# A three-stage convolution block: a written-out opening for the third stage with direct mean and variance products, first products ahead of a transpose, and other buffers for the last pieces

## The chip, the cores and the metric

The kernel runs on one core of one Trainium2 chip. The number that counts is the device time of one execution in microseconds (us), taken as the median of the runs shown. A core has a matrix engine (TensorE, "PE" in the profile, with "PEld" for its weight loads), a vector engine (VectorE, "DVE"), an activation engine (ScalarE, "ACT"), GpSimd ("POOL") and a synchronising engine ("SP"). SP, ACT and POOL also issue the DMA transfers. Each engine carries out its own instructions in the order written and waits on semaphores for the others.

## What is computed

The input is `x` of shape (16, 192, 64, 64), float32. Two layers follow each other (weights are cut away here):

```python
def layer0(x):
    h = ln2d(x)                                    # over the 192 channels, for every pixel
    projected, gate = split(conv1x1(h, in_proj))   # 192 -> 2 * 192
    projected = dwconv3(projected)                 # depthwise 3x3
    scanned = scan_lr + scan_rl + scan_tb + scan_bt    # four first-order recurrences, weighted
    mixed = (scanned + dwconv3(projected)) * sigmoid(gate)
    mixed = gelu(batch_norm(mixed))                # statistics over images and pixels
    x = x + conv1x1(mixed, out_proj)
    m = conv1x1(gelu(conv1x1(ln2d(x), fc1)), fc2)  # 192 -> 768 -> 192
    return x + m

def layer1(x):
    t = relu(bn(mean(x, pixels) @ w1.T))           # per image
    taps = (t @ w2.T + b2) * MASK                  # 4 taps of 9 are left by the mask
    return depthwise3x3(x, taps) + bias            # own taps for each image and channel
```

## The kernel before

The instruction order of all engines is the order of the Python text. The images are taken in eight pairs, one image on each half of the 128 partitions, with the 192 channels as three groups (`t` = 0, 1, 2) of 64.

**First stage** (lines 246 to 584): 64 chunks `n` of 512 pixels of a pair, four quarters `g` each. `load_a` brings a chunk (three transfers on SP, three on POOL), three chunks ahead. `turn(n)` transposes it on PE into PSUM (one buffer, `ps_xt`), `variance(n, g)` reads the per-pixel statistics from there on DVE, `deviation(n)` makes the reciprocal of the deviation, and `project(n)` multiplies by the weights `wi` into `ps_pj` (two buffers of each kind); DVE (line 517) and ACT (line 518) scale the two images' results into a staging block. The mean is taken out of the weights beforehand: `projection_weights` scales `wi`, makes its column means on PE (line 281) and subtracts them on DVE (line 284). Loop order: `turn(n + 1)`, then `project(n)` with the statistics of `n + 1` among its quarters. Four chunks make a block; blocks lie alternately in `stg` and in `mid`, and during the next block the four stores of a block go out on POOL and SP. So the first write of a block waits for the stores of the block two before. The table `side` puts small steps after given chunks: the weight loads after 40, 41, 43 and 44, and after chunks 46, 47, 48 and 49 `load_dm(0)`, `load_lm(0)`, `load_dm(1)`, `load_lm(1)`, which bring banded matrices for the second stage, each on SP for one half of the partitions and on POOL for the other (786 KB for a `dm`, 655 KB for a `lm`, by their tile shapes).

**Second stage** (587 to 789): 24 groups of eight channels; depthwise product, two scans on DVE, local product, gate. At the end of a group its result, 2 MB, goes to DRAM (`mixed_d`, line 704, one transfer on POOL). The last group lies in `mid`. For it, four small transfers (702) first put what chunk 0 of the next stage needs directly in its place. Then `spread` and `batch_norm` make the statistics while the DVE transposes (`turn_back`, 239) turn chunk 0.

**Third stage** (792 to 1096): 64 chunks `n` of 512 pixels again. The steps of a chunk:

- `unmix` (transposes, DVE), `bn_gelu` (852 and 853, ACT) make `mx`: parts 0 and 1 with 128 channels, part 2 with the other 64 channels;
- `out_proj(n, t)`: products over part 2 (880, "quarters" below) and then parts 0 and 1 (884, "columns"); `residual(n, t)` (890, DVE) adds the input into the image `ximg`; for `t` = 1 and 2 it also adds up the channels by thirds and halves (894, 905);
- `mean` (913): four products of these sums with a constant matrix; `center` (920) subtracts the mean; `squares` (927 ACT, 928 and 905 DVE) squares and adds; `mean` again for the variance;
- `normalize`: square root (936, ACT, with an activation-table load), `reciprocal` (939) and product (940) on DVE;
- `first(n, k)` for `k` = 0, 1, 2 (952, PE; GELU 954 on ACT) and `second(n, k)` (825 by way of `both`, PE); `final` (972) adds to the image.

The loop runs from `n` = -3 and overlaps four chunks: `first(n, 0)`, `products(n, 0)` (mean of `n + 1` and output product 0 of `n + 2`), `squares(n + 1)`, the last `second` of `n - 1`, `first(n, 1)`, `products(n, 1)` (variance of `n + 1`), `second(n, 0)`, `normalize(n + 1)`, `first(n, 2)`, `products(n, 2)`, `second(n, 1)`. The opening is the same loop with the missing chunks left out. In `products` mean and output product share a PSUM tile, `ps_o` ("f1", two buffers, also used by `first`). `load_y` brings `mixed_d` back, two chunks at a time; in the opening into the room of `ximg1`, which is empty until the second pair.

**The end** (1098 to 1118): the depthwise product of the last pair, twelve pieces of 1024 pixels and 64 channels. Five are made on ACT and DVE (1026 and 65), seven on PE (1035) with an eviction on ACT (1037). All twelve write into the four `gl` buffers in turn, and a buffer is free again when its transfer to DRAM has ended.

Of the kernel before, what the change touches and what calls it, by code (L numbers as in the profile page):

```python
# [27 lines left out]
C = 192  # L28
# [27 lines left out]
def conv_block_kernel(ctx: ExitStack, tc: tile.TileContext, x, prm, w_in, w_out, w_fc1, b_fc1, w_fc2, w1, bn1, w2, out):  # L56
# [103 lines left out]
    early = ExitStack()  # L160
    ce = early.enter_context(tc.tile_pool(name="early", bufs=1))
    ones = ce.tile([128, 128], F32, tag="ones", name="ones")

# [10 lines left out]
    mats[0]["lm"] = lm_even  # L174

    SB_ = 2 * 2 * C * BR
    mid = ce.tile([128, SB_], F32, tag="mid", name="mid")
    mats[1]["lm"] = mid[:, NPG:NPG + 5 * HW * (GC // 2)].rearrange("p (k m c) -> p k m c", k=5, m=HW)
# [67 lines left out]
    with ExitStack() as stage:  # L246
# [199 lines left out]
        for k in (0, 1, 3, 4):  # L446
            beside(40 + k, load_weights, k)
        beside(46, load_dm, 0)
        beside(47, load_lm, 0)
        beside(48, load_dm, 1)  # L450
        beside(49, load_lm, 1)
        beside(50, squeeze_scale)
# [46 lines left out]

        def project(n):  # L500
            blk, part = divmod(n, per)
            if part == 0:
                if blk % 2:
                    both_i = mid.rearrange("p (i o j) -> p i o j", i=2, j=BR)
                else:
                    both_i = stg.tile([128, 2, 2 * C, BR], F32, tag="stg", name="stg")
                stag[blk] = [both_i[:, i] for i in range(2)]
            for g in range(AR):
                ps = [psa.tile([128, 2 * C], F32, tag=f"pj{i}", name=f"ps_pj{i}", bufs=2) for i in range(2)]
                for t in range(3):  # L510
                    for i, q in enumerate(HALF):
                        nc.tensor.matmul(ps[i], pixels(n, t, g)[q], wi[q, t].rearrange("p g k c -> p (g k c)"),  # L512
                                         start=(t == 0), stop=(t == 2))
                if n + 1 < n_ac:
                    variance(n + 1, g)
                j, rs = part * AR + g, ast[n]["rs"]
                nc.vector.tensor_scalar_mul(stag[blk][0][:, :, j], ps[0], rs[:, g, 0:1])  # L517
                nc.scalar.activation(stag[blk][1][:, :, j], ps[1], AF.Copy, scale=rs[:, g, 1:2])  # L518
# [36 lines left out]
        next(steps)  # L555
        decays()
        turn(0)
        next(steps)
        for g in range(AR):
            variance(0, g)  # L560
        next(steps)
        deviation(0)

        for n in range(n_ac):
            if n + 3 < n_ac:
                load_a(n + 3)
            blk, part = divmod(n, per)
            if blk:
                if part == 0:
                    store_first(blk - 1)  # L570
                    store(blk - 1, 0, (nc.gpsimd, nc.sync))
                store(blk - 1, part + 1, (nc.gpsimd, nc.sync))
                if part == per - 1:
                    stag.pop(blk - 1)
            if n + 1 < n_ac:
                turn(n + 1)
            project(n)
            if n + 1 < n_ac:
                deviation(n + 1)
            for f, args in side.pop(n, ()):  # L580
                f(*args)
# [5 lines left out]
    with ExitStack() as stage:  # L587
# [98 lines left out]
        def gate(k):  # L686
# [9 lines left out]
            if c == hp_ - 1:  # L696
                if g == NCG - 1:

                    for i in range(2):
                        for wh in range(2):  # L700
                            w0_ = 32 * wh
                            (nc.sync, nc.gpsimd)[wh].dma_start(y_low[2 * w0_ + 32:2 * w0_ + 64, 2, i, LASTC * BR:],
                                                              s["pg"][w0_:w0_ + 32, i * NB, 0].rearrange("p c j -> p (c j)"))
                nc.gpsimd.dma_start(mixed_d[:, :, :, g].rearrange("i b p e -> p (i b) e"),
                                    s["pg"][:, :, 0].rearrange("p n c j -> p n (c j)"))
                s.clear()
# [89 lines left out]
    n_img = 2  # L796
    ximg = [k3.tile([128, 3, HW + 1, RW], F32, tag=f"ximg{i}", name=f"ximg{i}") for i in range(n_img)]

# [56 lines left out]
    def products(n, t):  # L855
# [4 lines left out]
        ps = ps2.tile([128, 2, CH], F32, tag="f1", name="ps_o", bufs=2)  # L860
        pm, po = ps[:, :, HCH:CH], ps[:, :, 0:HCH]
        if t < 2:
# [11 lines left out]
    def out_proj(n, t, ps):  # L874

        s = st[n]

        for wh, qr in enumerate(HALF):
            for i, q in enumerate(HALF):
                nc.tensor.matmul(ps[q, wh], wo2[qr, 64 * t:64 * t + 64], s["mx"][qr, 2, 256 * i:256 * i + 256],  # L880
                                 start=True, stop=False)
        for wh in range(2):
            for i, q in enumerate(HALF):
                nc.tensor.matmul(ps[q, wh].rearrange("p (r w) -> p r w", w=32), wo[:, 64 * t:64 * t + 64],  # L884
                                 cols(rows(s["mx"][:, i]))[:, :, wh], start=False, stop=True)

    def residual(n, t, ps):
        s, img = st[n], img_of(n)
        for wh in range(2):
            nc.vector.scalar_tensor_tensor(cols(img[:, t])[:, :, wh], ps[:, wh].rearrange("p (r w) -> p r w", w=32),  # L890
                                           pt3[:, t, OUTB:OUTB + 1], cols(rows(s["x2"][:, t]))[:, :, wh], ALU.add, ALU.add)
        if t == 1:
            s["sum"] = hp2.tile([128, 3, HCH], F32, tag="sm", name="sm", bufs=1)
            nc.vector.tensor_add(rows(s["sum"][:, 0:2].rearrange("p k n -> p (k n)")), img[:, 0], img[:, 1])
# [12 lines left out]
    def mean(n, ps, what):  # L907
# [3 lines left out]
        for k, kinds in enumerate(((s0, sx), (sx, s1))):  # L911
            for i, a in enumerate(kinds):
                nc.tensor.matmul(ps[HALF[i], k], mean64[HALF[k]], a[HALF[k]], start=True, stop=True)  # L913

    def center(n, pm):
# [101 lines left out]
    def dynamic_last(p, g, t, dg, queues=(nc.gpsimd, nc.sync)):  # L1017

        xi, taps, r = ximg[p % n_img], pst[p]["taps"], g * GR
        o = wp.tile([128, GR, HW], F32, tag="gl", name="ol", bufs=4)  # L1020
        src = lambda k, r0, nr: xi[:, t, r0 + k // 3:r0 + k // 3 + nr, k % 3:k % 3 + HW]
# [34 lines left out]

    for n in range(-3, n_ch + 1):
        ended = (n - 1) // NCH if n >= NCH and (n - 1) % NCH == NCH - 1 else None
        if n + 5 < NCH and (n + 5) % 2 == 0:
            load_y(n + 5, ys[(n + 5) // 2], (nc.sync, nc.gpsimd) if n == -3 else (nc.gpsimd,))  # L1060
        if n == -3:
            border(ximg[0])
        if n == 0:
            nc.vector.memset(pool2, 0.0)
        if n == NCH - 3:
            border(ximg[1])

        early_, late_ = (n + 3, None) if n != -1 else (None, 2)
        at(load, n + 3)
        at(unmix, early_)  # L1070
        at(load_mixed, n + 4)
        at(first, n, 0)
        at(bn_gelu, early_)
        products(n, 0)
# [19 lines left out]
        at(second, n, 1)  # L1094
        at(unmix, late_)
        at(bn_gelu, late_)

# [63 lines left out]
```

## Time and profile before

| | us |
|---|---|
| three runs | 3748.33, 3750.83, 3751.44; median 3750.83 |
| profiled execution | 3738.29, of which 3736.5 are the span of the profile |
| first stage, about | 0 to 636 |
| second stage, about | 636 to 1311 |
| third stage, about | 1311 to 3697 |
| end, about | 3697 to 3736.5 |
| busy over the span: PE, DVE, ACT, POOL | 3686.8, 2706.0, 1786.6, 420.2 |

The profile is of one execution. A line of a timeline has the start, the length, the engine, the line of the code, the operation with its operands, the number of merged instructions, and in brackets how long the engine was idle before and for whom it waited. A float32 matmul shows as two instructions. A line of windows has the bounds, the length, then busy time and number of instructions of each engine, the granted share of the TensorE clock, the DMA engines' share and GB/s.

### The profile page before, as it was taken

What the parts mean: (1) busy time and instruction counts of PE and PEld (TensorE: products, weight loads), DVE (VectorE), ACT (ScalarE), POOL (GpSimd) and SP (SyncE); (2) the same over time, 40 slices, a digit from 0 to 9 for tenths busy, and PEclk for the clock granted to TensorE, in tenths of its full rate; (3) what the DMA queues carried; (4) which work ended last, traced back from release to release, by engine and by line L of the source; (5) the groups of instructions that cost most, each with busy time, mean ns of one, the idle gap of its engine ahead of it and who ended that gap; (6) DMA issues with size and microseconds to landing.
All of it is one profiled execution on the core that took longest, in us unless ns stands there. A gap on an engine that the chain in (4) does not pass through costs nothing.

```text
span 3736.5 us, 71017 instructions
## 1 busy us (share of the span) xinstructions
PE 3686.8 (99%) x30252; PEld 1649.4 (44%) x30252; DVE 2706.0 (72%) x4164; ACT 1786.6 (48%) x1945; POOL 420.2 (11%) x683
## 2 busy tenths in 40 slices
PE   8999999999999979999999999999999999999998
PEld 5666656555555533333333333333333333333333
DVE  6887776999999965557666766766766766675763
ACT  3434434888888833334334434434443443443432
POOL 2334332101011020000000000000000000000000
PEclk9999999999999989999999999999999999999999
DMA  6899997999999841112212222222222221221212
GB/s 163 241 252 243 265 280 238 308 294 283 280 283 271 226 100 27 51 44 63 78 56 66 69 67 62 69 61 68 74 57 58 76 71 42 80 75 43 69 37 74
DMA packets 308427, 491.74 MB, mean 132 GB/s; under 512 B 46656, under 2 KB 202640, under 8 KB 308112
## 3 DMA queue, kind: packets, MB, share of 16 engines
q1 hardware_dynamic: 250064, 295.14, 29.5%
q0 software_dynamic: 57152, 190.94, 18.7%
q8 instruction: 239, 3.92, 0.4%
q10 hardware_dynamic: 896, 1.12, 0.1%
q14 instruction: 76, 0.62, 0.1%
HBM read 284.91 MB, written 197.92 MB: 129 GB/s over the span
## 4 chain that ended last, share of the span: by engine, by line
PE 96%; DMA 2%; DVE 1%; SPq 0%; POOL 0%; issue 0%; ACT 0%; ACTq 0%; DVEq 0%; POOLq 0%
PE ps_f L952 27%; PE ps_f L825 27%; PE ps_pj L512 12%; PE ps_l L662 11%; PE ps_d L618 7%; PE ps_o L884 5%; PE ps_xt L484 2%; PE ps_o L880 2%; PE ps_o L913 1%; DMA xa<-in_x_dram 1%; PE ps_k L825 0%; DMA ximg<-mixed_d 0%; DMA mixed_d<-mid 0%; SPq L472 0%; PE ps_d L1035 0%
## 5 line engine op out<-in xcount | busy, mean ns | idle before, releaser
L954 ACT ACTIVATE gl<-ps_f,bf 128x1024 f32<-128x1024 f32 x384 | 427.6, 1114 | 1316.2 <-PE ps_f L952 1316.2
L952 PE MATMUL ps_f<-h,wf 64*64 64x512 f32 x9216 | 1035.8, 594 | 6.8 <-DVE h L940 6.7
L825 PE MATMUL ps_f<-gl,place 128*64 128x512 f32 x4608 | 1022.2, 592 | 0.0
L952 PEld LDWEIGHTS ps_f<-h,wf 64*64 64x64 f32 x9216 | 334.5, 133 | 693.8 <-issue 642.6
L825 PEld LDWEIGHTS ps_f<-gl,place 128*64 128x64 f32 x4608 | 334.2, 137 | 574.5 <-issue 533.4
L512 PE MATMUL ps_pj<-wi,xa 64*128 64x384 f32 x3072 | 515.6, 488 | 3.5 <-DVE stg L517 3.5
L920 DVE TENSOR_TENSOR h<-ximg,ps_o 128x768 f32<-128x768 f32 x128 | 116.4, 951 | 425.3 <-PE ps_o L884 417.0
L512 PEld LDWEIGHTS ps_pj<-wi,xa 64*128 64x128 f32 x3072 | 294.3, 187 | 196.8 <-issue 12.2
L890 DVE SCALAR_TENSOR_TENSOR ximg<-ps_o,pt,low 128x256 f32<-128x256 f32 x384 | 168.0, 479 | 266.8 <-PE ps_o L884 266.8
L65 DVE SCALAR_TENSOR_TENSOR o<-ximg,taps,o 128x1024 f32<-128x1024 f32 x252 | 323.2, 1282 | 9.1 <-ACT o L1011 2.6
L1015 POOL DMA_DIRECT2D out_dram<-o x168 | 87.9, 528 | 2067.6 <-DVE o L65 2064.8
L939 DVE RECIPROCAL rs<-rs 128x512 f32<-128x512 f32 x64 | 214.3, 3349 | 27.0 <-ACT rs L936 27.0
L653 DVE TENSOR_TENSOR_SCAN v<-tab,q 128x1024 f32<-128x1024 f32 x96 | 218.3, 2274 | 6.8 <-ACT tab L641 6.8
L655 DVE TENSOR_TENSOR_SCAN v<-tab,q 128x1024 f32<-128x1024 f32 x96 | 217.5, 2266 | 0.0
L518 ACT ACTIVATE stg<-ps_pj,rsa 128x384 f32<-128x384 f32 x128 | 120.5, 945 | 188.7 <-PE ps_pj L512 178.5
L884 PE MATMUL ps_o<-low,wo 128*64 128x256 f32 x1536 | 210.0, 395 | 0.0
L641 ACT ACTIVATE tab<-mask,dec_b 128x1024 f32<-128x1024 f32 x192 | 209.8, 1146 | 0.0
L518 ACT ACTIVATE mid<-ps_pj,rsa 128x384 f32<-128x384 f32 x128 | 120.8, 944 | 181.7 <-PE ps_pj L512 174.7
L491 DVE BATCH_NORM_STATS2 st<-ps_xt 128x6 f32<-128x192 f32 x512 | 173.8, 340 | 17.3 <-PE ps_xt L484 17.1
L239 DVE STREAM_TRANSPOSE low<-low 128x512 f32<-128x512 f32 x174 | 167.7, 1016 | 2.1 <-issue 0.3
L972 DVE SCALAR_TENSOR_TENSOR ximg<-ps_f,pt,ximg 128x512 f32<-128x512 f32 x192 | 134.4, 749 | 40.2 <-PE ps_f L825 37.8
L472 POOL DMA_DIRECT2D xa<-in_x_dram x192 | 119.8, 630 | 362.6 <-PE ps_pj L512 285.0
(197 smaller groups left out, 4060.1 us busy)
## 6 DMA issues: line engine op xcount, KB each, us to landing
low<-in_x_dram SPq DMA_DIRECT2D x128, 384.0 KB
out_dram<-o POOLq DMA_DIRECT2D x168, 256.0 KB, 3.7
mid<-pg_d SPq DMA_DIRECT2D x8, 4096.0 KB
low<-mixed_d SPq DMA_DIRECT2D x116, 256.0 KB
low<-pg_d SPq DMA_DIRECT2D x7, 4096.0 KB
pg_o<-pg_d SPq DMA_DIRECT2D x7, 4096.0 KB
xa<-in_x_dram POOLq DMA_DIRECT2D x192, 128.0 KB, 5.6
xa<-in_x_dram SPq DMA_DIRECT2D x192, 128.0 KB
```

The source lines that it names most:

```text
L65: nc.vector.scalar_tensor_tensor(o, in0, scalar, in1, ALU.mult, ALU.add, **kw)
L512: nc.tensor.matmul(ps[i], pixels(n, t, g)[q], wi[q, t].rearrange("p g k c -> p (g k c)"), start=(t == 0), stop=(t == 2))
L518: nc.scalar.activation(stag[blk][1][:, :, j], ps[1], AF.Copy, scale=rs[:, g, 1:2])
L618: nc.tensor.matmul(dst(ps[o, ih]), mats[g % 2]["dm"][q, di + 1, :, ch], src(s["pg"][q, :, 0, ch]), start=(di == 0), stop=stop)
L653: nc.vector.tensor_tensor_scan(vf, tab, q, 0.0, ALU.mult, ALU.add)
L655: nc.vector.tensor_tensor_scan(vf[:, ::-1], tab[:, ::-1], q[:, ::-1], 0.0, ALU.mult, ALU.add)
L662: nc.tensor.matmul(dst(bst[k]["ps"][o, i]), lm_of(g)[q, m, :, c], src(q, ih), start=start, stop=stop)
L825: nc.tensor.matmul(ps[q], w(i), rhs(i), start=start, stop=stop)
L884: nc.tensor.matmul(ps[q, wh].rearrange("p (r w) -> p r w", w=32), wo[:, 64 * t:64 * t + 64], cols(rows(s["mx"][:, i]))[:, :, wh], start=Fa ...
L939: nc.vector.reciprocal(rs, rs)
L952: nc.tensor.matmul(pf[o, i], wf1[q, t, m0:m0 + 64], s["h"][q, t], start=(t == 0), stop=(t == 2))
L954: nc.scalar.activation(gl, pf, AF.Gelu, bias=bf1[:, m:m + 1])
```

## The change

- First stage: the means of `wi` are made and subtracted before `turn(0)`. For chunk 0 the first two quarters are projected before `turn(1)`, the other two after it with two statistics steps each. `load_dm` and `load_lm` stand after chunks 46, 48, 50, 52, in the order dm 0, lm 0, dm 1, lm 1.
- `mid` is the first tile of its pool, and `ximg1` is placed before `ximg0`. In the built program `mid` then has the addresses of `ximg1`, and no address in common with `ximg0`.
- The 2 MB store of the last group is two transfers of 1 MB, one on SP and one on POOL.
- The third stage's loop starts at `n` = 1. What lay before is written out. For chunk 0 the columns stand before the quarters, and the sums on DVE are left out: mean and variance come from twelve products each, straight from the image and from the squares. They have a PSUM bank of their own. The squares are made in two halves, and the square-root table is loaded right after them. `normalize(0)` stands before `residual(1, 1)` on DVE.
- The pieces of the end that ACT and DVE make write into the `o` buffers (three pieces) and the `h2` buffers (two); the four `gl` buffers are left to the seven PE pieces.

```diff
@@ first stage
-        beside(46, load_dm, 0)
-        beside(47, load_lm, 0)
-        beside(48, load_dm, 1)
-        beside(49, load_lm, 1)
+        for i in range(2):
+            beside(46 + 4 * i, load_dm, i)
+            beside(48 + 4 * i, load_lm, i)
...
         decays()
+        next(steps)
+        next(steps)
         turn(0)
-        next(steps)
         for g in range(AR):
             variance(0, g)
-        next(steps)
         deviation(0)
...
+            h = AR // 2 if n == 0 else 0
+            project(n, range(h), lambda g: ())
             if n + 1 < n_ac:
                 turn(n + 1)
-            project(n)
+            project(n, range(h, AR), lambda g: (g,) if h == 0 else (2 * (g - h), 2 * (g - h) + 1))
@@ store of the last group
+                parts = ((nc.gpsimd, 0, n_half),) if g < NCG - 1 else ((nc.sync, 0, n_half // 2), (nc.gpsimd, n_half // 2, n_half))
+                for queue, i0, i1 in parts:
+                    queue.dma_start(mixed_d[i0:i1, :, :, g].rearrange("i b p e -> p (i b) e"),
+                                    s["pg"][:, i0 * NB:i1 * NB, 0].rearrange("p n c j -> p n (c j)"))
@@ third stage
+    def mean_part(n, pm, t, k, src):
+        for i, q in enumerate(HALF):
+            nc.tensor.matmul(pm[q, k], mean64[q], src[q], start=(t == 0 and k == 0), stop=(t == 2 and k == 1))
...
+    load_y(2, ys[1], (nc.sync, nc.gpsimd))
+    border(ximg[0])
+    for n in range(2):
+        load(n)
+        unmix(n)
+        bn_gelu(n)
...
+    for t in range(3):
+        out_alone(0, t)
+        if t:
+            for k in range(2):
+                mean_part(0, pm, t - 1, k, img0[:, t - 1, halves[k]])
+    for k in range(2):
+        mean_part(0, pm, 2, k, img0[:, 2, halves[k]])
+    center(0, pm)
+    load(2)
...
+    for k in range(2):
+        nc.scalar.activation(sq0[:, k], st[0]["h"].rearrange("p t (k n) -> p k t n", k=2)[:, k], AF.Square)
+    nc.scalar.activation(warm, eps6, AF.Sqrt)
+    out_alone(1, 0)
+    pw = one_bank()
+    for k in range(2):
+        for t in range(3):
+            mean_part(0, pw, t, k, sq0[:, k, t])
+    st[0]["pw"] = pw
+    normalize(0)
+    load_y(4, ys[2], (nc.gpsimd,))
+    residual(1, 1, out_alone(1, 1, True))
+    out_alone(1, 2)
+    first(0, 0)
+    pm = ps2.tile([128, 2, CH], F32, tag="f1", name="ps_o", bufs=2)[:, :, 0:HCH]
+    mean(1, pm, "sm")
+    unmix(2)
+    center(1, pm)
+    bn_gelu(2)
+    squares(1)
+    load(3)
+    first(0, 1)
+    unmix(3)
+    out_alone(2, 0)
+    second(0, 0)
+    bn_gelu(3)
+    products(0, 1)
+    normalize(1)
+    first(0, 2)
+    products(0, 2)
+    second(0, 1)
+    nc.vector.memset(pool2, 0.0)
+
+    for n in range(1, n_ch + 1):
@@ the end, dynamic_last
+        if dg is None:
+            o = (op.tile([128, GR, HW], F32, tag="o", name="o") if g < 2 else
+                 hp2.tile([128, 3, CH], F32, tag="h2", name="ol")[:, 0:2].rearrange("p k (h w) -> p (k h) w", w=HW))
+        else:
+            o = wp.tile([128, GR, HW], F32, tag="gl", name="ol", bufs=4)
```

`out_alone` is an output product with its residual (without it where `later` is set, in two `f2` banks of its own).

## The prediction

> **What bounds the kernel now.** I read the busy shares first: PE 99%, so only idle or slowed PE time can be won. Then windows by stage, to find where it idles:
>
> ```profile
> 21.50:300.00 278.50, 278.45 (x1805) 176.52 (x1804) 222.65 (x724) 111.20 (x149) 100.82 (x169) 1.00 0.83 219
> 430.00:500.00 70.00, 66.62 (x412) 42.19 (x410) 48.16 (x144) 25.69 (x35) 27.56 (x47) 0.98 0.97 282
> 1300.00:1320.00 20.00, 10.89 (x92) 6.13 (x89) 17.40 (x23) 9.87 (x10) 2.81 (x3) 0.72 0.42 113
> 1320.00:1345.00 25.00, 15.07 (x102) 6.43 (x98) 13.76 (x24) 5.77 (x7) 14.58 (x27) 0.81 0.82 167
> 1400.00:3640.00 2240.00, 2240.00 (x17430) 829.43 (x17426) 1475.54 (x2046) 905.35 (x871) 87.98 (x169) 1.00 0.23 61
> 3640.00:3736.50 96.50, 85.41 (x650) 31.61 (x642) 37.79 (x53) 29.27 (x27) 5.18 (x10) 0.94 0.26 75
> ```
>
> The second column of numbers is the length, the third PE's busy time: no gap in 1400 to 3640, and the order there is untouched. What can move lies at 9 to 30, at 430 to 500, at 1306 to 1348 and after 3697. Third, PE's and DVE's timelines through the opening of the third stage:
>
> ```profile
> 1318.18 1.13 PE L880 MATMUL ps_o<-low,wo 64*64 64x256 f32 x8 [3.84 <-ACT low L853]
> 1326.56 1.69 PE L913 MATMUL ps_o<-sm,mean 64*64 64x256 f32 x7 [1.53 <-DVE sm L905]
> 1334.69 1.95 PE L913 MATMUL ps_o<-sq,mean 64*64 64x256 f32 x6 [4.79 <-DVE sq L905]
> 1340.30 1.08 PE L884 MATMUL ps_o<-low,wo 128*64 128x256 f32 x8
> 1348.09 7.91 PE L952 MATMUL ps_f<-h,wf 64*64 64x512 f32 x48 [6.71 <-DVE h L940]
> 1371.08 5.38 PE L952 MATMUL ps_f<-h,wf 64*64 64x512 f32 x48
> ...
> 1321.80 0.88 DVE L890 SCALAR_TENSOR_TENSOR ximg<-ps_o,pt,low 128x256 f32<-128x256 f32 x2 [2.02 <-PE ps_o L884]
> 1329.96 1.82 DVE L920 TENSOR_TENSOR h<-ximg,ps_o 128x768 f32<-128x768 f32 x2 [2.19 <-PE ps_o L884]
> 1342.79 3.35 DVE L939 RECIPROCAL rs<-rs 128x512 f32<-128x512 f32 x1 [1.36 <-ACT rs L936]
> ```
>
> PE waits on one dependent chain for chunk 0: products, residual, mean, centre, squares, variance, root, reciprocal. It ends at 1348.09, and the first 48 instructions then take 7.91 us instead of 5.38. The other two places, PE in the first stage and ACT at the end:
>
> ```profile
> 489.60 5.83 PE L512 MATMUL ps_pj<-wi,xa 64*128 64x384 f32 x24 [3.04 <-DVE stg L517]
> ```
> ```profile
> 3730.58 1.11 ACT L1037 ACTIVATE ol<-ps_d,pt 128x1024 f32<-128x1024 f32 x1 [2.75 <-DMA out_dram<-ol]
> ```
>
> The first waits for a staging block whose last store was issued by SP at 480.14 and landed at 488.62 (chain of waits); the second for a `gl` buffer.
>
> **Part A, first chunk: -2.4 us.** Now the six mean products start when the weights are scaled (9.23) instead of at 14.61: 9.3 + 4.2 (the row of line 281) = 13.5. The last piece of chunk 0 is in at 13.46 (chain), so `turn(0)` follows: 2.8 (the row of 12 transposes at 18.75) gives 16.3; with 1.53 (warm row at 29.69) or 3.26 (three cold rows of 1.09) it would be 15.0 or 16.8. Eight statistics steps of 0.47: 20.1. Meanwhile PE makes two quarters, 24 instructions of 0.167 (8.01 for 48): 20.3; `turn(1)` to 21.8, its input having been there at 18.75 before. Root and reciprocal (0.6), two scalings (0.9 each) to 22.5, four statistics steps 24.4, scaling 25.3, four steps 27.2. `turn(2)` begins at 27.3, against 29.69. Ends: 3.7, and 0 if the next chunks are not in that early.
>
> **Part B, the banded matrices: -2.0 us.** `load_lm(0)` moves from after chunk 47 to after 48, `load_dm(1)` to 50, `load_lm(1)` to 52. On SP and POOL they now pass the loads and stores of these chunks, each of which goes out one or two transfers earlier. The matrices are first used from 640 on, over 100 us later. The late store at 480.14 stood behind the same SP transfers, but POOL's half of `lm` 0 (327 KB, issued at 474.91) no longer shares the DMA with it: 327 KB at 282 GB/s is 1.2 us. The clock's share of this stall is 5.83 - 4.14 (the same 24 at 334.73) = 1.7; after an idle time of 0.41 nothing of it was paid, after 3.04 all, so I take half, 0.85. Ends: 0 and 3.04 + 1.7 = 4.7.
>
> **Part C, the opening: -8.2 us.** Columns first: they need only line 852 (ends 1317.42), where the quarters needed 853 (1318.13): -0.7. Three products lasted from 1318.18 to 1325.02, 6.84; one set of four mean products now stands among them. A set puts two products on the array at a time, as line 884 does (1.01 warm), so 1.01; bounds 0.43 (eight of line 913) and 1.95. 1317.47 + 6.84 + 1.01 = 1325.3; the second set to 1326.3 while DVE makes the last residual (0.88); third set 1327.35; centre at 1327.45, against 1329.96. The store of `mid` does not matter much here: the first residual began at 1321.80 because that store ended at 1321.71, and in the built program it still lists a wait for both halves, though the addresses are now apart; it has slack, since the set that needs it starts at 1322.6. The split itself I cost at nothing: in 1315 to 1319 the DMA share was already 0.97 and 1.00.
>
> Then: first half of the centre 0.95, 1328.4; half square 0.9 (between 0.80 for 512 elements at line 853 and 1.24 for 1024), 1329.3, the other 1330.2; variance products 1.5 each half (three pairs of 0.5), 1330.9 and 1332.4; the table load (1.28 + 0.2) ends at 1331.7 beneath them; root 0.69 to 1333.2; reciprocal 3.35, product 1.76 and 0.1 between them: 1338.4. `first(0, 0)` starts at 1338.5 instead of 1348.09: -9.6. Cover for the longer variance products: nothing, they are on the path; the sums they replace (0.69 + 1.77 twice) were too. The residuals of chunk 1 now stand behind the product on DVE.
>
> What is late next: `first(0, 1)` has only `mean(1)` (0.43) before it where mean and output product stood, and its PSUM buffer waits for the GELU of the second half: 1.1 + 0.2 - 0.43 = 0.9 lost. `unmix(2)` stands ahead of `center(1)` on DVE, with the second buffer of `first(0, 1)` behind it: residuals, sums and transposes 0.88 + 0.69 + 0.88 + 1.77 + 3.0 = 7.2, to 1345.6, centre to 1347.5; PE wants that buffer at about 1350. Without `second(0, 0)` between, the second buffer of `first(0, 2)` waits for the root of chunk 1: about 0.5. So 9.6 - 1.4 = 8.2. PE idles from 1335.4 (two output products after 1332.4) to 1338.5, 3.1 us; I assume that the clock falls, as in this row after 3.04. Ends: 5.1 (mean and variance sets at the cold rate, + 3.1) and 12.5 (sets at 0.43, and the clock stays up).
>
> The Trainium skill ("TensorE: Matmul & The Clock Gate", Part 1) says that the clock falls after an idle window of about 3.4 us. By that rule 3.1 us of idleness would leave it up and the sum would be 2.65 larger, 17.4; the first-stage row above (3.04 idle, then slow) decides for me.
>
> **Part D, the end: -2.2 us.** Seven PE pieces need PE from 3701.95; four took 15.52, to 3717.47, and three at 3.58 end at 3728.2 without the gaps 0.17 and 0.64 at 3717.64 and 3725.38. The last eviction then starts at 3728.3 instead of 3730.58, and the 4.8 us from its end to the span's end stay. SP gets the stores of the DVE pieces earlier, and their fifth ends near 3724.7, ahead of that. Ends: 0.8 and 2.3.
>
> **Sum.** 2.4 + 2.0 + 8.2 + 2.2 = 14.8. Against the profiled execution 3738.29 - 14.8 = 3723.5; the median of the runs lies 12.5 higher, which I carry over: 3750.83 - 14.8 = **3736.0 us**.
>
> **Rivals.**
> - *The clock stays up* before `first(0, 0)`: 2.65 more, and the half cold price in B, 0.85: 3732.5. For it: 3.1 is an estimate, and in 1306 to 1309 the clock share was 0.98 with PE idle from 1306.4. Against: 0.50 from 1309 on, 2.6 us after.
> - *The clock stays down through the whole opening*: C falls to 5.1, and the late warm-up costs another 2.5 in `first(0, 1)`: total 9.2, 3741.6. Against: 1.00 in 1324 to 1332 with fewer products.
> - *The opening's gain is handed back to the transfers* of `load_y(2)`: `unmix(2)` asks at 1342.6, not at 1350.57, and holds `center(1)` behind it. Were the data there only at 1350.5, C would be nothing, 6.6 would be left, 3744.2: no change. Against: these 24 transfers landed 2.5 to 3.6 us after issue, the last about 1332. The same holds if the built order leaves the old wait on the path.
> - *Slower*: the matrices moved to chunks 50 and 52 meet the stores of the next blocks, and PE stalls at each block boundary, chunks 48, 52, 56 and 60, for 8.0 each, halfway between the stall of before (4.7) and the longest transfer in the chain of that stage (11.34, `xa` at 303.30): 32.0 - 4.7 = +27.3, less A, C and D (12.8), +14.5: 3765.3. It decides from a DMA share near 1.0 after chunk 48 on; 500 to 636 shows 0.83 and 243 GB/s, which should drain.
>
> **Chances.** Forecast 0.57, clock up 0.18, clock down 0.10, handed back 0.08, slower 0.07. A difference below 0.2% (7.5 us) can't be told from no change here. Faster is the first three, 0.85; same 0.09 (the fourth, and a mild form of the last); slower 0.06. The range 3728 to 3745 takes in the ends of all four parts but for their coincidence, and all cases but the last.
>
> **What would show it.** Right: first `ps_f` product near 1338 less what A and B moved it (about 1334), twelve-product sets near 1.0 each four, no idle PE beyond 1 us until the steady rhythm, no wait for `out_dram<-ol` at line 1037's counterpart, a stall after chunk 48 below 2 us. Wrong: a DMA wait ahead of `turn(1)`, new waits for `stg` or `mid` at later blocks, or DVE waiting for `ximg<-mixed_d`.

## The result and the profile after

| | before | after |
|---|---|---|
| runs, median (lowest to highest), us | 3749.58 (3746.79 to 3751.44), 4 runs | 3725.53 (3720.6 to 3734.31), 4 runs |
| profiled execution, us (its span) | 3738.29 (3736.5) | 3720.6 (3718.8) |

The ratio is 0.9939, 95% interval [0.9918, 0.996]: faster by 24 us, and by 15 to 31 with the interval. A second group of runs with another copy of the same kernel gave 3727.87 (5 runs) against 3746.5 (9 runs), 0.9949 [0.9937, 0.9962], so 14 to 24 us. The prediction had the sign and the places right and said 14.8; the time lies 2.5 below the low end of its range.

The windows of the kernel after, in the columns explained for before (bounds, length, busy time and instructions of PE, PEld, DVE, ACT and POOL, clock, DMA share, GB/s):

```profile
21.50:300.00 278.50, 277.77 (x1804) 176.32 (x1804) 223.14 (x732) 110.27 (x150) 104.18 (x173) 1.00 0.86 224
300.00:360.00 60.00, 57.68 (x364) 35.90 (x362) 42.45 (x125) 22.98 (x32) 22.91 (x38) 0.97 1.03 249
430.00:500.00 70.00, 69.88 (x447) 43.22 (x444) 52.95 (x158) 28.38 (x38) 26.41 (x46) 1.00 1.01 292
1314.92:1339.92 25.00, 21.30 (x184) 10.33 (x180) 16.89 (x24) 7.27 (x10) 14.93 (x27) 0.89 0.91 164
1400.00:3625.00 2225.00, 2225.00 (x17308) 823.60 (x17308) 1467.95 (x2041) 898.88 (x864) 88.12 (x169) 1.00 0.23 61
```

430 to 500 has lost its gap (66.62 of 70 busy before), and the opening, 5.08 earlier as a whole, has PE busy for 21.30 of 25 instead of 15.07. But 300 to 360 now has a gap of 2.3 that the first profile of before hardly had.

PE's timeline of the kernel after, in the first stage and in the opening of the third; the columns are start, length, engine, line, operation, number of instructions, and the idle time before with its releaser:

```profile
8.54 4.20 PE L281 MATMUL pb<-wi,wf 64*128 64x384 f32 x6 [8.54 <-DVE wi L277]
12.68 2.82 PE L483 MATMUL ps_xt<-ident,xa 128*128 128x128 f32 x12
...
26.37 1.50 PE L483 MATMUL ps_xt<-ident,xa 128*128 128x128 f32 x12 [0.69 <-PE ps_pj L512]
333.29 5.84 PE L512 MATMUL ps_pj<-wi,xa 64*128 64x384 f32 x24 [2.32 <-DVE stg L517]
...
1317.71 1.05 PE L938 MATMUL ps_m<-ximg,mean 64*64 64x256 f32 x8
...
1324.47 2.56 PE L938 MATMUL ps_m<-sq,mean 64*64 64x256 f32 x21 [0.57 <-ACT sq L1122]
...
1333.33 7.08 PE L977 MATMUL ps_f<-h,wf 64*64 64x512 f32 x48 [3.00 <-DVE h L965]
...
1341.63 5.38 PE L977 MATMUL ps_f<-h,wf 64*64 64x512 f32 x48 [0.79 <-ACT gl L979]
...
1358.71 2.81 PE L977 MATMUL ps_f<-h,wf 64*64 64x512 f32 x24 [0.33 <-ACT rs L961]
```

The third transpose starts at 26.37 (29.69 before). The idle time at 333.29 is chunk 32's: PE waits for DVE, and DVE for leave to write the staging block `stg`, as at 489.60 before. By the program only that block's stores can hold it, and SP issues the last of them at 324.29; the profile puts DVE's wait down to a load of `xa`, so that it is the store is inferred:

```profile
332.38 0.86 DVE L517 TENSOR_SCALAR stg<-ps_pj,rsa 128x384 f32<-128x384 f32 x1 [4.39 <-DMA xa<-in_x_dram]
```

In the opening the direct products (L938) stand between the output products; the waits of 4.79 and 6.71 are gone, one of 3.00 is left, and the two new small ones (0.79 for the GELU, 0.33 for the root) are those that the prediction named. DVE's side of the same opening:

```profile
1315.51 0.88 DVE L908 SCALAR_TENSOR_TENSOR ximg<-ps_o,pt,low 128x256 f32<-128x256 f32 x2 [0.79 <-PE ps_o L895]
...
1322.51 1.82 DVE L945 TENSOR_TENSOR h<-ximg,ps_m 128x768 f32<-128x768 f32 x2 [1.19 <-PE ps_m L938]
...
1328.04 3.35 DVE L964 RECIPROCAL rs<-rs 128x512 f32<-128x512 f32 x1 [2.92 <-ACT rs L961]
1331.42 1.76 DVE L965 TENSOR_TENSOR h<-h,rs 128x1536 f32<-128x1536 f32 x1
```

From the centre (1322.51) to the reciprocal it takes 5.53; before it took 12.83 (1329.96 to 1342.79).

The end. First PE's 48 small products `ps_k` of the last pair's tap weights, in the kernel before and then in the kernel after (same inputs, same idle time ahead):

```profile
3698.48 2.72 PE L825 MATMUL ps_k<-red,w2t 48*64 48x1 f32 x48 [0.62 <-DVE red L991]
```

```profile
3683.53 1.56 PE L831 MATMUL ps_k<-red,w2t 48*64 48x1 f32 x48 [0.62 <-DVE red L1016]
```

Then ACT's last evictions in the kernel after:

```profile
3708.68 1.11 ACT L1066 ACTIVATE ol<-ps_d,pt 128x1024 f32<-128x1024 f32 x1 [2.45 <-PE ps_d L1064]
3710.85 2.00 ACTq L1073 DMA_DIRECT2D out_dram<-ol  x2
3712.98 1.11 ACT L1066 ACTIVATE ol<-ps_d,pt 128x1024 f32<-128x1024 f32 x1 [3.19 <-DMA out_dram<-o]
```

PE is done without a gap (26.06 us from 3685.84, so at 3711.90), but the last eviction is behind ACT's own issue of the store before it, which lasts until 3712.85, and starts 1.1 later than PE would allow. The profile puts this wait down to a transfer of `o`; but in all ten profiles with the buffers of after the last eviction starts 0.12 to 0.13 after that issue ends.

### The profile page after: what moved, and what is told of

It is laid out like the page before. It is cut to its first block, busy times and chain, and to the rows that moved or that the text cites. A ratio compares the mean times of both kernels' runs of the same rounds, so it can differ in the third digit from the quotient of the medians.

```text
span 3718.8 us, 71068 instructions
## 1 busy us (share of the span) xinstructions
PE 3683.1 (99%) x30284; PEld 1836.7 (49%) x30284; DVE 2698.7 (73%) x4154; ACT 1785.6 (48%) x1947; POOL 420.2 (11%) x683
## 4 chain that ended last, share of the span: by engine, by line
PE 98%; DVE 1%; DMA 1%; ACT 0%; issue 0%; SPq 0%; ACTq 0%; DVEq 0%
PE ps_f L977 27%; PE ps_f L831 27%; PE ps_pj L512 14%; PE ps_l L665 11%; PE ps_d L621 7%; PE ps_o L902 5%; PE ps_xt L483 2%; PE ps_o L895 2%; PE ps_o L933 1%; PE ps_d L1064 0%; DMA xa<-in_x_dram 0%; PE ps_k L831 0%; DVE v L658 0%; DMA place<-in_w_in_dram 0%; DVE v L656 0%
## 5 line engine op out<-in xcount | busy, mean ns | idle before, releaser
L512 PEld LDWEIGHTS ps_pj<-wi,xa 64*128 64x128 f32 x3072 | 292.8, 188 | 197.0 <-issue 12.6
L65 DVE SCALAR_TENSOR_TENSOR o<-ximg,taps,o 128x1024 f32<-128x1024 f32 x261 | 334.6, 1282 | 9.3 <-ACT o L1036 2.6
L490 DVE BATCH_NORM_STATS2 st<-ps_xt 128x6 f32<-128x192 f32 x512 | 173.3, 338 | 12.6 <-PE ps_xt L483 12.4
```

Source lines behind the costliest of these rows:

```text
L65: nc.vector.scalar_tensor_tensor(o, in0, scalar, in1, ALU.mult, ALU.add, **kw)
```

## The experiments

Times are medians; a ratio is to the runs of the kernel before that were made beside it, with its 95% interval. All kernels were profiled too. Since one execution can't be compared with another as a whole (the kernel before ran from 3737.85 to 3755.37 in 30 runs), I read distances inside a profile: the start of turn(2) (the third transposes) for part A; the idle time at chunk 48 for B; from `pm`, the first of the products that add up the batch norm's statistics at the end of the second stage, to the first `ps_f` product of chunk 1, first(1, 0), for C; and from `ps_t` (L988 of before) to the end for D.

### Each part alone

a_only is before with the first stage's edit:

```diff
-        turn(0)
         next(steps)
+        next(steps)
+        turn(0)
         for g in range(AR):
             variance(0, g)
-        next(steps)
...
+            h = AR // 2 if n == 0 else 0
+            project(n, range(h), lambda g: ())
             if n + 1 < n_ac:
                 turn(n + 1)
-            project(n)
+            project(n, range(h, AR), lambda g: (g,) if h == 0 else (2 * (g - h), 2 * (g - h) + 1))
```

b_only is before with the loads of the banded matrices spread:

```diff
-        beside(46, load_dm, 0)
-        beside(47, load_lm, 0)
-        beside(48, load_dm, 1)
-        beside(49, load_lm, 1)
+        for i in range(2):
+            beside(46 + 4 * i, load_dm, i)
+            beside(48 + 4 * i, load_lm, i)
```

c_only is before with the opening of the third stage, the places of `mid` and `ximg`, and the store in two halves:

```diff
+        if n == 0:
+            out_columns(n, t, ps, True)
+            out_quarters(n, t, ps, False)
...
+    for k in range(2):
+        for t in range(3):
+            mean_part(0, pw, t, k, sq0[:, k, t])
```

d_only is before with other buffers for the last pieces:

```diff
-        o = wp.tile([128, GR, HW], F32, tag="gl", name="ol", bufs=4)
+        if dg is None:
+            o = (op.tile([128, GR, HW], F32, tag="o", name="o") if g < 2 else
+                 hp2.tile([128, 3, CH], F32, tag="h2", name="ol")[:, 0:2].rearrange("p k (h w) -> p (k h) w", w=HW))
+        else:
+            o = wp.tile([128, GR, HW], F32, tag="gl", name="ol", bufs=4)
```

> The kernel before with the first-stage edit alone (column means and first two quarters ahead of the transposes). Theory 1, the gain is handed back: turn(2) starts about 3 us earlier, and the staging block of chunk 32 waits that much longer, so that the second stage starts within 1 us of before and the time stays within 2 us. Rival, the gain is kept: 2.4 to 3.3 us faster.

> The kernel before with the banded matrices' loads after chunks 46, 48, 50, 52 alone. Theory 1: the stall at chunk 48 goes in every run, and it is in most runs larger than the 4.7 us of the profiled one: 8 to 12 us faster, with no new stall at chunk 52. Rival, as the two profiles differ: 5.4 us faster. Rival, as predicted: 2.0.

> The kernel before with the opening of the third stage alone (order written out, direct products, places of mid and ximg, split store). Both theories: first(0, 0) starts 9.7 us earlier than the end of the second stage before it would let it, and 9.9 are left at first(1, 0). Time 9 to 11 us faster; 12 or more would say that the clock or the transfers of the opening vary from run to run.

> The kernel before with the other buffers for the ACT and DVE pieces alone. As predicted: 2.2 us faster. By the profile after: 1.6, because the last eviction then waits for ACT's own issue of transfers instead of a buffer.

Measured, beside before at 3747.81 (30 runs):

| kernel | median, us (runs) | ratio | gain by the ratio, us |
|---|---|---|---|
| a_only | 3743.34 (12) | 0.9988 [0.9976, 1.0] | 4.5 |
| b_only | 3745.01 (11) | 0.9996 [0.9987, 1.0005] | 1.5 |
| c_only | 3734.37 (7) | 0.9966 [0.9954, 0.9979] | 12.7 |
| d_only | 3746.43 (12) | 0.9995 [0.9986, 1.0005] | 1.9 |

The four sum to 20.6, and the whole change gave 24 and 18.6 in its two groups: the parts neither eat nor feed each other by more than the spread. The order is that of the prediction, but C and A are larger than it had them. B and D alone can't be told from nothing by the times, and A only just. Two theories among the expectations failed: A's gain is not handed back at chunk 32 (4.5 alone, against at most 2), and B alone is worth 1.5 and not 8 to 12. The "12 or more" of c_only came, and with it the suspicion that the clock of the opening varies.

### The whole change again, and with one part undone

no_a is after with the first stage's order of before, no_b is after with the loads of the matrices after chunks 46 to 49; the diffs are those above, read backwards.

> The changed kernel once more, as the yardstick of this group. Theory 1, run-to-run spread comes from the stalls of the first stage: the second stage starts anywhere from 630 to 643 us, while from there to first(0, 0) and from first(1, 0) to the end everything repeats within 1 us (27.4 us from the last statistics product to first(0, 0)). Rival, the opening itself varies: that 27.4 changes by more than 1. Time 20 to 25 us below before.

> The changed kernel with the first-stage edit undone (transposes first again), all else kept. Theory 1, handed back at chunk 32: within 2 us of the changed kernel. Rival, kept: 2.4 to 4.5 us slower than it.

> The changed kernel with the loads of the banded matrices put back after chunks 46, 47, 48, 49, all else kept. If the spread is worth what the two first profiles differ by, 5 us slower than the changed kernel with a stall at chunk 48; if it is worth what its single run gave, 1 to 2 us.

Beside before at 3746.5 (9 runs): after_again 3727.87 (5 runs), 0.9949 [0.9937, 0.9962]; no_a 3732.19 (5), 0.9961 [0.9948, 0.9973]; no_b 3725.87 (5), 0.9953 [0.9939, 0.9966]. Undone in the changed kernel, A costs 4.5 and B 1.5 by the ratios: the same two numbers as alone. But the intervals overlap, and by the plain medians no_b is 2.0 below after_again; B's worth rests on the profiles. The 18.6 of after_again is below the 20 to 25 expected of it.

The profiles say why A is more than its 2.4. turn(2) started at 29.69, 30.59, 30.91, 30.51 and 29.54 in the five kernels without A (before, b_only, c_only, d_only, no_a; mean 30.25), and at 25.26 to 26.96 in the nine with it (mean 26.29): 3.96 earlier. For B: PE's idle time ahead of chunk 48's product was 3.04, 1.79, 1.23, 0.87 and 0.90 in the five without it (before, a_only, c_only, d_only, no_b; mean 1.57), and none in six of the nine with it, then 0.32, 0.43 and 2.22 (mean 0.33). That is 1.2 of idle time, and the clock fell in one execution of each kind.

after_again showed something that had not been foreseen. In the opening the first `ps_f` product came 27.91 after `pm` (27.41 in the first profile of after), with the same 3.00 us of idle PE, and yet the clock had not fallen:

```profile
1342.94 5.38 PE L977 MATMUL ps_f<-h,wf 64*64 64x512 f32 x48 [3.00 <-DVE h L965]
```

no_a gave 5.38 there too, c_only, no_b and apart 7.08. One program, one idle time, two prices; the next runs took that up.

### What the direct products are worth: sums

after, with the mean and the variance of chunk 0 by DVE's sums and four products, all else kept:

```diff
-    for k in range(2):
-        for t in range(3):
-            mean_part(0, pw, t, k, sq0[:, k, t])
+    pw = two_banks()
+    mean(0, pw, "sq")
```

> The kernel after, but the mean and the variance of chunk 0 go the old way: DVE adds the three thirds up (0.69 and 1.77 us each time) and four products follow, in a two-bank tile; order of the opening, places, split store and all other parts stay. Theory (the direct products are a part of the gain of their own): the centre starts up to 2.3 later than in the kernel after, the variance takes 6.3 to 7.7 from the start of the centre instead of 4.8, so the first ps_f product starts about 2.5 later, 30 us after pm instead of 27.4 to 27.9; PE is then idle for well over 3.0, its clock falls for sure and the first 48 instructions take 7.9 instead of 5.4 to 7.1. At first(1, 0) 3 us are lost, and the time is about 3 above the kernel after. Rival (the order and the places alone bring it, the sums hide in waits that DVE has anyway): the first ps_f product stays within 0.5 of 27.4, time as after.

3727.41 (6 runs), 0.9948 [0.9936, 0.996] beside before at 3747.79 (11 runs). PE's timeline of sums:

```profile
1326.44 1.69 PE L931 MATMUL ps_o<-sm,mean 64*64 64x256 f32 x7 [1.55 <-DVE sm L923]
...
1333.12 1.95 PE L931 MATMUL ps_o<-sq,mean 64*64 64x256 f32 x6 [3.33 <-DVE sq L923]
...
1341.46 5.38 PE L975 MATMUL ps_f<-h,wf 64*64 64x512 f32 x48 [0.86 <-DVE h L963]
```

`pm` started at 1311.16, so the first `ps_f` product comes 30.30 after it, 2.4 to 2.9 later than in after (27.41 and 27.91), as expected. Of the 9.7 us by which C moves this product, the direct products bring a bit over a quarter; order and places bring the rest. The price of the clock was not as expected: the long idle time now lies ahead of the variance products, the clock falls there and is up again when `ps_f` starts. At first(1, 0) sums is 63.32 after `pm`, after 62.12 and after_again 60.92: 1.2 to 2.4 lost, and not 3. By the times (3727.41, beside 3724.73 and 3724.48 of one_store and fill in its group) the loss can't be told, since the intervals overlap.

### What the halved store is worth: one_store

after, with the last group's store of `mixed_d` as one transfer of POOL:

```diff
-                parts = ((nc.gpsimd, 0, n_half),) if g < NCG - 1 else ((nc.sync, 0, n_half // 2), (nc.gpsimd, n_half // 2, n_half))
+                parts = ((nc.gpsimd, 0, n_half),)
```

> The kernel after, with the last group's store of mixed_d as one POOL transfer instead of an SP and a POOL half. Theory (the split is worth nothing, as the prediction costed it): the first residual, 9.6 us after pm in the kernel after and put down to PE, begins at most 1.2 later, the slack before the third set of output products takes it, and the first ps_f product stays within 0.3 of 27.4 to 27.9; time as after within 1. Rival (the built wait for this store is on the path): the first residual begins 10.8 after pm as in the kernel before, and the first ps_f product about 1.2 later.

3724.73 (6 runs), 0.9946 [0.9932, 0.9959]. The first residual starts 10.81 after `pm`, as late as before (10.80), and no longer 9.59; the first `ps_f` product starts 27.44 after `pm`, as in after (27.41). The store does hold the first residual, and the slack of the next products takes it all: the split is worth nothing, which is what the prediction charged for it.

### The idle time filled: fill

after, plus six products whose result is not used, in a free bank while PE waits:

```diff
     out_alone(1, 2)
+    fill = ps2.tile([128, CH], F32, tag="f2", name="ps_fill", bufs=3)
+    for _ in range(3):
+        both(fill, lambda i: wf1[:, 0, 0:64], lambda i: wf1[:, 0, 0:CH], True, True)
     first(0, 0)
```

> The kernel after, with six 64x512 products of wf1 with itself into a free bank, their result unused, just before first(0, 0). They add work and keep PE busy for 1.3 to 2.6 of the 3.00 us of idle time there. Theory (the idle time costs the clock, and that price is 7.08 - 5.38 = 1.7): idle time ahead of the first ps_f product below 2, its 48 instructions take 5.38 to 5.5 in every execution, first(0, 0) starts at the same 27.4 to 27.9 after pm, and first(1, 0) 60.9 to 61.1 after pm instead of 62.1, as in the one execution of after in which the clock stayed up; 1 us of 3726. Rival (first(0, 1) then only waits longer for its GELU): the 48 take 5.38 but first(1, 0) stays at 62. The excite's 48 small products stay at 1.56 if their place in PSUM made them fast; if the distance to the last change of the clock did, they may be 2.72 again.

3724.48 (5 runs), 0.9943 [0.9929, 0.9956]: no difference from one_store (3724.73) in the same group. In the profile the fill works where it stands (idle 0.42, 48 instructions in 5.38, first(1, 0) at 59.59 after `pm`). The 59.59 is not the fill's alone: here the clock came up 9.53 after `pm`, against 11.20 in after, and the first `ps_f` product stood at 26.58 instead of 27.41. In best, with the same fill, the clock came up at 12.27, and first(1, 0) is at 60.89. But `ps_k` (the excite's products of the expectation), at the other end of the kernel, takes 2.72 again:

```profile
3683.92 2.72 PE L831 MATMUL ps_k<-red,w2t 48*64 48x1 f32 x48 [0.62 <-DVE red L1016]
```

Its buffers are those of after, where it took 1.56. So their place in PSUM, which had been one possible reason, is not it. The clock is, and the windows show how. I cut the opening of three executions into stretches of 3.413 us, beginning where a change of the clock fell. First after, then after_again, then one_store:

```profile
1330.78:1334.19 3.41, 0.86 (x8) 0.42 (x12) 3.34 (x5) 0.00 (x0) 0.00 (x0) 1.00 1.18 145
1334.19:1337.60 3.41, 3.41 (x20) 1.29 (x16) 3.25 (x8) 0.00 (x0) 0.69 (x1) 0.50 0.70 101
1337.60:1341.01 3.41, 3.24 (x36) 1.27 (x28) 2.69 (x4) 1.66 (x2) 2.02 (x3) 1.00 1.10 150
```

```profile
1337.62:1341.03 3.41, 2.32 (x24) 0.88 (x20) 3.35 (x1) 1.49 (x2) 0.00 (x0) 1.00 0.99 153
1341.03:1344.45 3.42, 1.51 (x16) 0.78 (x20) 3.38 (x5) 0.00 (x0) 0.00 (x0) 1.00 1.17 117
1344.45:1347.86 3.41, 3.41 (x37) 1.45 (x32) 3.25 (x7) 1.11 (x1) 2.30 (x4) 1.00 0.66 133
```

```profile
1341.24:1344.65 3.41, 1.32 (x16) 0.49 (x8) 3.38 (x2) 0.50 (x2) 0.66 (x2) 1.00 0.98 124
1344.65:1348.06 3.41, 2.50 (x12) 0.88 (x16) 3.34 (x7) 0.00 (x0) 0.00 (x0) 0.50 1.20 143
1348.06:1351.48 3.42, 3.42 (x20) 1.10 (x16) 3.30 (x7) 0.47 (x1) 0.84 (x2) 0.50 1.01 102
```

The second number is PE's busy time, the third from the end the clock. In after the idle time of 3.00 fell almost whole into one stretch (0.86 busy): the next stretch ran at 0.50, was busy throughout, and the one after it ran at full speed; price 7.08 - 5.38 = 1.70. In after_again the same idle time was cut in two by the border, 2.32 and 1.51 stayed busy, and nothing fell. In one_store the clock fell after 1.32; the stretch after the fall had 2.50 of work, and the clock stayed down for a second one: the 48 took 8.29, price 2.91.

At the end of the kernel the same grid matters. From first(1, 0) to `ps_t` it is 2314.43 in before and after and 2314.44 in fill and after_again, which is 678 of these stretches and 0.2: where the grid stands in the opening, it stands at the end. In after the clock falls at 3685.97, when `ps_k` is over; in before at 3698.20, ahead of it. So the opening and the end trade. From `pm` to first(1, 0) plus from `ps_t` to the end it is 62.12 + 36.33 = 98.45 in after, where the clock fell in the opening, and 60.92 + 37.31 = 98.23 in after_again, where it did not. The same sum is 98.21 to 98.45 in the five profiles of the whole change without the fill that keep the split store and the direct products (after, after_again, no_a, no_b, apart), 98.38 in best and 97.02 in fill. So what the fill saves in the opening is in one profile lost again at the end, and in the other 1.2 to 1.4 are left, which the times can't show; that the trade is why the fill moves no time fits these numbers but is not shown.

### Stores of the side vectors apart: apart, and best

The idle time at chunk 32 was there in all twelve profiles of kernels with the old order of the side vectors, 0.41 in before and 2.26 to 6.37 in the others. Ahead of it SP and POOL send stores of `lv_d` in small pieces, of two vectors at once. apart is after with these spread, so that they no longer overlap at chunks 27 and 28, and later, so that fewer lie before chunk 32; best is apart with the fill.

```diff
-        for k, n in enumerate((9, 11, 13, 15, 19, 24, 28, 32)):
+        for k, n in enumerate((9, 11, 13, 15, 19, 26, 30, 34)):
```

> The changed kernel with the vectors 5, 6 and 7 of the second stage's coefficients made after chunks 26, 30, 34 instead of 24, 28, 32, so that the stores of two of them (pieces of 16 bytes) no longer fall on the same chunks 27 and 28, and fewer lie before chunk 32. Theory 1: the stall at chunk 32 (2.3 to 4.0 us idle and up to 1.7 at the slow clock in every profile but the first) comes from SP lagging behind these stores and goes: 3 to 6 us faster than the changed kernel. Rival, the stall comes from the sheer amount of data: the same time, a stall at chunk 32 or 36.

> The kernel after with both the fill of the run above and side-vector stores that no longer overlap at chunks 27 and 28 (the last three groups end at chunks 26, 30, 34 instead of 24, 28, 32). Theory: the gains of the two add, 5 to 6 from the stores (3720.8 against 3725.9 to 3727.9 in their group) and 1 from the fill: 3719 to 3720, ratio to before 0.993. Rival: the gain of the stores was one of chance between executions, and the time is 3726 as the kernel after.

apart: 3720.78 (5 runs, 3718.64 to 3723.77), 0.9932 [0.9919, 0.9944]; best: 3720.44 (6 runs), 0.9929 [0.9915, 0.9942]. In neither profile is there idle time at chunk 32. In after SP's issue of three loads behind these stores took 11.84, and the last store of the staging block went out at 324.29; in apart it took 6.39, and the store went out at 319.43. So SP was late in after; whether the overlap or the number of the stores before chunk 32 made it late the runs don't part, since apart changes both. In each one stall is left elsewhere, here that of apart:

```profile
409.85 5.83 PE L512 MATMUL ps_pj<-wi,xa 64*128 64x384 f32 x24 [2.71 <-DVE stg L517]
```

apart is 7.1 below after_again and 5.1 below no_b of its group, best 4.0 and 4.3 below fill and one_store of its own. The intervals of the ratios overlap in both groups; the two groups agree. These two have the lowest times here, and no gain of the fill can be told between them.

## Why the prediction was partly wrong

Its forecast, range and carry: it took the profiled execution (3738.29) for the working and carried over the 12.5 us by which the median lay above it. This is the largest step that failed. The median of after lies 4.9 above its profiled execution and not 12.5: of the 10.5 us by which 3736.0 was too high, 7.6 lie there, and 2.9 in the sum (the two profiled executions differ by 17.7). The first stage differs between the profiles by 12 us (its end lies between 630.48 in after and 642.94 in c_only), and by 11 between two with the same first stage, after and one_store (641.49), of which the idle time at chunk 32, 2.32 and 6.37, makes up 4.05. The profile of before, with 0.41, showed least of this idle time. Which execution was profiled is luck, and the range had no term for it: the upper ends of all four parts together, 3.7 + 4.7 + 12.5 + 2.3 = 23.2, are less than the 24.05 timed. The sum of terms, 14.8, stands against 18.6 and 24.05 timed; by distances inside the profiles it should have been about 20:

| term | predicted | by the profiles | by the times |
|---|---|---|---|
| A, first chunk | 2.4 | 3.96 | 4.5, 4.5 |
| B, matrices | 2.0 | 1.2 idle | 1.5, 1.5 |
| C, opening, up to first(1, 0) | 8.2 | 10.70 | |
| C and D, from `ps_t` on | 2.2 | 3.73 | |
| C alone, D alone | 8.2, 2.2 | 12.6, 2.6 | 12.7, 1.9 |
| sum | 14.8 | 19.6 | 18.6, 24.05 |

10.70 is the mean of before, a_only, b_only and d_only (72.42) less that of c_only, after, after_again, no_a, no_b and apart (61.72). 3.73 is the mean of before, a_only and b_only (40.41) less that of after, after_again, no_a, no_b and apart (36.68). C alone is the 10.70 and the 1.91 from 40.41 to c_only's 38.50; D alone is 40.41 less d_only's 37.78. The three that make 40.41 lie between 39.08 and 41.08, and c_only and d_only are one profile each, so these two hold to about 1 us.

- *C, the term of the sum that failed most.* The prediction's chain held: the first `ps_f` product was to come 9.6 earlier and came 9.68 earlier (37.09 and 27.41 after `pm`); the two new stalls were to cost 1.4 and showed as 0.79 + 0.33. What was mis-sized is the clock. "I assume that the clock falls, as in this row after 3.04" took one price, and the same as before, for a thing that has three (5.38, 7.08, 8.29 for the same 48 instructions after the same 3.00). In the profiles without C the first 48 took 7.91 to 8.10, so 0.8 to 2.7 more came back in the profiles of c_only, after, after_again, no_a, no_b and apart than the sum had, on the mean 1.5 (8.03 and 6.51); with the next 48 (5.68 and 5.38) that is 1.8 of the 2.5 that C's front was mis-sized by. And the sum had no term for `ps_k` at all: it took 2.72 or 2.73 in the four profiles without C and 1.56 to 1.66 in nine of the ten with it, 1.16 less at the best. In three of the nine the clock fell while `ps_k` ran, and the end is about 1 us longer there (after_again 37.31, no_a 37.42; after, no_b and apart 36.06 to 36.33).
- *The rival that the clock stays up* was right in two of the seven executions with an idle time of 3.00. Its 2.65 is not worked out; the rows give 7.91 - 5.38 = 2.53. In this case's windows the clock fell after a stretch with 0.86 and one with 1.32 us of work and stayed up after one with 1.51, so the stretch need not be idle, and an idle time can't be held against 3.4 by its length. The Trainium skill ("TensorE: Matmul & The Clock Gate", Part 1) speaks of a free-running window of 4096 cycles at 1.2 GHz, 3413 ns. The grid of 3.413 agrees with it. The same section lets the clock fall after an idle window, which is not what these stretches show.
- *A: "`turn(2)` begins at 27.3".* It began at 26.37. The products of the mean were ready at 8.54, not 9.3, because the first third of the scaled weights is enough to start, and the transposes followed at 12.68 with no wait for the last piece. The other 0.6 is in the 29.69 of before, the second best of five.
- *B* went where it was said to go and was about as large; its ends (0 and 4.7) hold every reading. The landing at 488.62 that it names is, in the chain of waits, that of a load of `xa`; that the store held the block is inferred. The slower rival, stalls at chunks 48 to 60, did not come: the largest at chunk 48 with the matrices spread is 2.22.
- *D: "The last eviction then starts at 3728.3".* That is 26.35 after the first `ps_d` product (3701.95); it started 27.14 after it (28.63 before). The stall for `gl` is gone from PE, but the prediction left out ACT's own queue, where the issue of the store before takes 2.00; the size still came out at 1.9 to 2.6.
- *Handed back to load_y(2)*: DVE waits nowhere for `ximg<-mixed_d` in the opening of after, as forecast.
- *The signs.* The first `ps_f` product came at 1333.33 (about 1334 forecast) and a set of four mean products took 1.05 (1.0). "No idle PE beyond 1 us" did not come, 3.00 was left, as the prediction's own working had it (3.1); and the last eviction still has a wait of 3.19.

What is not shown: why the stall at chunk 32 varies as it does, what sets the position of the grid at the end of the second stage, and how much work in a stretch keeps the clock up.

## What to carry to other kernels

Don't take a cold clock as a fixed price of an idle time: lay the 3.413 grid over the profile, and range the price from nothing to two stretches at half speed, up to 2.9 us here. Read a small change in distances inside several profiles, from a mark just ahead of the edit to one just behind it, since whole executions here differ by more than the edit is worth. When the front of a long PE-bound stretch moves, look at the far end too: a dependent tail there can win or lose by the clock without being touched.

## What the runs showed of the hardware

- The clock changes only on a fixed grid. Stretches of 0.1 us put the changes of before at 1308.88, 1322.52, 1332.76, 1339.59, 1346.41 and 1353.24: 4, 3, 2, 2 and 2 times 3.413 apart; and the next one, at 3698.20, is 687 times 3.4133 behind the last. In after it is 1303.47, 1317.12, 1334.19, 1337.60 and 3685.97.
- Ahead of the first `ps_f` products a stretch with 0.86 (after) or 1.32 (one_store) us of PE work was followed by half speed, one with 1.51 was not (after_again); at half speed a stretch with 2.50 of work did not raise the clock (one_store), while a full one did (after, and the second one of one_store).
- These numbers are no threshold for other places. In before a stretch with 1.62 was followed by the fall at 3698.20, and in after one with 2.04 by the fall at 3685.97. In after even a stretch that was busy throughout, 631.05 to 634.46, was followed by half speed. In the last two, one-column products (`ps_k`, and line 140's `pb_h`) make up most of the work, so PE's busy time alone does not say when the clock falls.
- Both prices appear in one program: after and after_again are the same kernel, with 7.08 and 5.38 for the same 48 instructions.
